# A pre-norm attention and feed-forward block on one core: the first slot's order of maxima, LayerNorm, value products and small transposes

## The chip, the cores and the metric

The kernel runs on one core of one Trainium2 chip. The metric is the device time of one execution in microseconds. The numbers are float32 throughout.

## The reference

For 4 sequences (batches) of 512 tokens and width 512: LayerNorm, attention with 32 query heads of 16 columns in groups of four that share 8 key and value heads, rotary embedding, a causal softmax, an output product, a residual sum, then LayerNorm again, a gated feed-forward layer of 1376 columns and a second residual sum.

```python
q = q * cos + _rotate_half(q) * sin
k = k * cos + _rotate_half(k) * sin
att = jnp.einsum('bhgqd,bhkd->bhgqk', qg, k) / math.sqrt(D_HEAD)
att = jnp.where(causal, att, -jnp.inf)
probs = jax.nn.softmax(att, axis=-1)
ctx = jnp.einsum('bhgqk,bhkd->bhgqd', probs, v)
...
x = x + attention(_layernorm(x), Wq, Wk, Wv, Wo)
x = x + (silu(xt @ W_gate.T) * (xt @ W_up.T)) @ W_down.T   # xt = _layernorm(x)
```

## The kernel before

**Order.** Every engine executes its instructions in the order in which the program issues them; no planner moves them. Tiles of a pool are reused in turn, and an instruction that needs a tile, or a bank of the accumulator memory (PSUM), waits until its last reader is done. The SyncE queue (SP) issues all loads concerned here.

**Banks.** Of the eight PSUM banks four hold scores (two pairs, `pairs[0]` and `pairs[1]`), one the value products (`av`), and three go in turn to everything else through `bank()` (L160): projections, transposes, the feed-forward layer.

**Head groups.** The 32 heads of a batch are cut into 8 groups of 4 heads. The softmax needs the row maximum ahead of the exponential, so each group's scores are computed twice. `scores` (L436) makes them row by row in three rounds; after each round `greatest` copies pair 1 to SBUF on ScalarE (`copy`, L447) and takes the maxima on VectorE, of pair 0 from PSUM, then of pair 1 from the copy (L454). `lowered` (L471) transposes the maxima on TensorE and VectorE adds them to the queries (`qa`, L472). `lowered_scores` (L480) makes the transposed scores with the maximum taken off, ScalarE takes the exponential into `e` (`probabilities`, L487), GpSimd (POOL) masks it (L491), and `averages` (L509) multiplies by the values.

**The pipeline.** The loop in `slot` runs over a batch's 8 groups. While group g has its lowered scores, exponentials and value products, group g+1 has its scores and maxima, in the same four banks. Between these steps `gap()` puts work of other stages, from a list of steps with costs: after gap n the cost done is the sum of the first n shares. In slot 0 the list holds the projections of batches 1, 2 and part of 3; in later slots the feed-forward layer of the batch before.

**The steps of a projection.** `begin` loads the input tiles (L243) and puts LayerNorm items on the deque `aside`; `norm` takes statistics on VectorE (L175 to L177), a power on POOL (L178) and scales on VectorE (L183). `do(aside)` issues one such item. `turned` transposes the normalised tiles (L195) and copies them to `xnT`, on VectorE (L198) for odd tiles and ScalarE (L200) for even ones. A product (L220; L275 for values) comes in two halves from `halved`; after the second, `finish` reads the bank at once: for queries and keys `rotated` (L228 and L230 on VectorE, L229 and L231 on POOL), for keys also `spread` (L260, L262, by way of `aside`), for values a copy on ScalarE (L284). `masked` (L421) makes `qa` on POOL.

**Prologue.** Ahead of slot 0 the program loads batch 0 and the weights, makes batch 0's keys, queries and values, and the first group's scores and maxima. `later` and `later_act` hold the scaling of finished groups (L519 to L533).

Of the kernel before, what the change touches and what calls it, by code (L numbers as in the profile page):

```python
# [21 lines left out]
P = 128  # L22
# [52 lines left out]
def preln_block_kernel(  # L75
# [81 lines left out]
    def load_w(t, src):  # L157
        nc.sync.dma_start(out=t, in_=src.rearrange("(k p) m -> p k m", p=P))

    def bank():  # L160
        return ps_mm.tile([P, T], F32, tag="mm", name="mm")

# [29 lines left out]
    def transposed(xn, i, xnT):  # L192
        pt = bank()
        for k in range(NK):
            nc.tensor.transpose(pt[:, ts(k, P)], xn[:, ts(k, P)], ident)  # L195
        src = pt.rearrange("p (k q) -> p k q", k=NK)
        if i % 2:
            nc.vector.tensor_copy(xnT[:, :, ts(i, P)], src)  # L198
        else:
            nc.scalar.copy(xnT[:, :, ts(i, P)], src)  # L200

    def halved(products, finish):

        made = {}

        def one():
            made["ps"] = bank()
            for step in products[: len(products) // 2]:
                step(made["ps"])

        def two():
            for step in products[len(products) // 2 :]:
                step(made["ps"])
            finish(made["ps"])

        return one, two
# [223 lines left out]
    def greatest(g, at, lo, hi):  # L440
# [6 lines left out]
        nc.scalar.copy(copy[:, :, lo:hi], pairs[1][:, :, lo:hi])  # L447
        for pair, src in enumerate((pairs[0], copy)):
            for i, c in at:
                n = P * (i + 1)  # L450
                for r in range(2):
# [10 lines left out]
                        accum_out=low[hf][:, i, row : row + 1],  # L462
                    )

    def lowered(g):
# [77 lines left out]


    for i in range(NT):
        load_xr(0, i)
    load_w(wk_sb, wk)
    nc.sync.dma_start(out=rope_sb, in_=rope)
    load_w(wq_sb, wq)
    load_w(wv_sb, wv)  # L550
    load_w(wo_sb, wo)

# [4 lines left out]
    begin[1]()  # L557
    do(aside, len(aside))
    for t in low:
        nc.gpsimd.memset(t, 0.0)  # L560
    for n in range(4):
        nc.gpsimd.memset(values(n), 1.0)
    for cost, step in turned:
        step()
    begin1[1]()
    for cost, step in start[:4]:
        step()
# [4 lines left out]
    rounds = (((3, 0),), 0, T), (((2, 0), (0, 3 * P)), 0, T), (((1, 2 * P),), 2 * P, T)  # L572
    scores(0, rounds[0][0])
    greatest(0, *rounds[0])
    do(aside, 3)
    for cost, step in start[6:8]:
        step()
    scores(0, rounds[1][0])
    greatest(0, *rounds[1])
    do(aside, 2)  # L580
    for cost, step in (turned1[0], *start[8:10], turned1[1]):
        step()
    scores(0, rounds[2][0])
    greatest(0, *rounds[2])
    for cost, step in (*turned1[2:], *start[10:]):
        step()
    masked(1)
    lowered(0)

    def fill(steps, upto, done):  # L590
# [6 lines left out]
    def slot(b, steps):  # L597
# [3 lines left out]

        shares = [0.19, 0.17, 0.19, 0.2, 0.25]
        done, part, n = 0.0, 0.0, 0

        def gap():
            nonlocal done, part, n
            part += shares[n % 5]
            n += 1
            done = fill(steps, total * part / 8, done)

        for g in range(8 * b, 8 * b + 8):
# [4 lines left out]
            do(later)  # L616
            do(aside)
            gap()
# [8 lines left out]
            do(later)  # L627
            do(aside)
            gap()
            at, lo, hi = rounds[1]  # L630
            scores(g + 1, at)
            greatest(g + 1, at, lo, hi)
            gap()
            at, lo, hi = rounds[2]
# [5 lines left out]
            gap()  # L640
            lowered(g + 1)
            averages(g)
        for cost, step in steps:
# [16 lines left out]

    slot(0, [begin2, *rest1, *turned2, begin3, *rest2, *turned3, *rest3[:-4]])

# [60 lines left out]
```

## Time and profile before

| | |
|---|---|
| median of 3 runs | 989.39 us (989.32 to 993.88) |
| profiled execution | 993.68 us, of which the span 992.0 |
| TensorE busy | 926.5 us (93%), mean granted clock 0.979 |
| VectorE busy | 535.8 us (54%) |
| ScalarE busy | 296.6 us (30%) |
| GpSimd busy | 216.0 us (22%) |

The engines' busy times are sums over the whole span, in which stages with different limits follow one another. In the page's slices the span is cut into 40 parts of 24.8 us, each digit the busy share in tenths. The prologue ends at 52.6 us of the span and slot 0 at 225.3; slots 1 to 3 and the last feed-forward layer follow. PE is TensorE, DVE VectorE, ACT ScalarE, POOL GpSimd. In an answer in order of time a row has start and duration in us, engine, line, operation, output and inputs; in brackets, the idle time of the engine before it and what ended it.

### The profile page before, as it was taken

The page shows a single profiled execution, that of the slowest core. Times are in us where ns is not written, and L with a number is a line of the kernel's source. Part 1 is how long each engine was busy: PE and PEld are TensorE (multiplying, and loading weights), DVE is VectorE, ACT ScalarE, POOL GpSimd, SP SyncE. Part 2 cuts the span into 40 slices and gives each one's busy share as a digit, 9 for nine tenths or more (in the row PEclk, how much of TensorE's full clock was granted, in tenths as well). Part 3 has the DMA queues.
Part 4 walks back from the last instruction along what each step waited for, and adds up shares of the span by engine and source line. Part 5 has one row for each costly group of instructions (what it writes and reads, how often), then busy time and mean ns, then how long its engine had stood idle before and what let it go on. Part 6 is the DMA issues. An engine that isn't in the chain of part 4 may idle for free.

```text
span 992.0 us, 12710 instructions
## 1 busy us (share of the span) xinstructions
PE 926.5 (93%) x4800; PEld 412.3 (42%) x4800; DVE 535.8 (54%) x1488; ACT 296.6 (30%) x385; POOL 216.0 (22%) x291
## 2 busy tenths in 40 slices
PE   6779887889899999999999999999999999999998
PEld 3334343443344444444444444444444443444443
DVE  5766677767665656475555564655655553312110
ACT  0134344443334333333333433323333431010000
POOL 5353354443311111212111111111111111100000
PEclk9898899999899999999999999999999999999999
DMA  6100100000244310040112110101212102022100
GB/s 212 43 1 1 34 11 1 2 1 1 65 159 126 84 45 26 11 170 11 53 45 53 43 50 11 54 1 43 54 43 54 41 19 64 11 75 75 47 11 32
DMA packets 56813, 46.63 MB, mean 47 GB/s; under 512 B 6352, under 2 KB 48336, under 8 KB 56496
## 3 DMA queue, kind: packets, MB, share of 16 engines
q1 hardware_dynamic: 56464, 40.05, 13.9%
q10 hardware_dynamic: 288, 5.77, 1.5%
q8 instruction: 38, 0.62, 0.3%
q14 instruction: 23, 0.19, 0.1%
HBM read 38.73 MB, written 7.08 MB: 46 GB/s over the span
## 4 chain that ended last, share of the span: by engine, by line
PE 77%; DVE 10%; ACT 5%; issue 2%; POOL 1%; DVEq 0%; ACTq 0%; POOLq 0%
PE mm L375 31%; PE mm L401 15%; PE sc L480 8%; PE av L509 8%; PE sc L436 7%; DVE junk L454 6%; PE mm L327 5%; ACT e L487 5%; PE mm L471 1%; PE mm L220 1%; DVE inv L532 1%; DVE st L175 0%; PE mm L195 0%; ACT xnT L200 0%; DVE inv L528 0%
## 5 line engine op out<-in xcount | busy, mean ns | idle before, releaser
L375 PE MATMUL mm<-xnT,shared 128*128 128x512 f32 (+1 forms) x704 | 324.2, 606 | 2.5 <-ACT xnT L200 2.5
L487 ACT ACTIVATE e<-sc 128x1024 f32<-128x1024 f32 (+1 forms) x192 | 160.6, 881 | 281.0 <-PE sc L480 268.0
L454 DVE CUSTOM_DVE_ANT_0 junk<-sc,mask 128x512 f32<-128x512 f32 (+3 forms) x256 | 125.6, 490 | 130.7 <-PE sc L436 94.1
L491 POOL TENSOR_SCALAR_AFFINE_SELECT e<-e 128x512 f32<-128x512 f32 x128 | 83.9, 667 | 512.8 <-issue 240.6
L375 PEld LDWEIGHTS mm<-xnT,shared 128*128 128x128 f32 (+1 forms) x704 | 126.2, 188 | 166.5 <-issue 159.0
L401 PE MATMUL mm<-wd_sb,home 128*128 128x512 f32 (+1 forms) x352 | 158.5, 599 | 0.0
L454 DVE CUSTOM_DVE_ANT_0 junk<-copy,mask 128x512 f32<-128x512 f32 (+3 forms) x256 | 131.2, 513 | 19.7 <-DVE low L454 0.5
L447 ACT COPY copy<-sc 128x1024 f32<-128x1024 f32 (+1 forms) x96 | 83.6, 871 | 194.7 <-PE sc L436 172.0
L480 PE MATMUL sc<-qa,home 32*128 32x512 f32 (+3 forms) x1024 | 96.3, 468 | 12.4 <-DVE low L454 10.2
L436 PE MATMUL sc<-home,qa 32*128 32x512 f32 (+3 forms) x1024 | 94.3, 460 | 10.7 <-ACT e L487 10.0
L401 PEld LDWEIGHTS mm<-wd_sb,home 128*128 128x128 f32 (+1 forms) x352 | 64.9, 190 | 82.7 <-issue 81.6
L509 PE MATMUL av<-e,home 128*32 128x512 f32 (+3 forms) x1024 | 80.7, 459 | 0.0
L480 PEld LDWEIGHTS sc<-qa,home 32*128 32x128 f32 x1024 | 43.3, 184 | 81.6 <-DVE low L454 54.3
L384 DVE SCALAR_TENSOR_TENSOR g<-g,mm 128x512 f32<-128x512 f32 (+1 forms) x44 | 30.2, 686 | 86.5 <-ACT g L383 86.5
L436 PEld LDWEIGHTS sc<-home,qa 32*128 32x128 f32 x1024 | 47.2, 187 | 64.8 <-issue 21.0
L327 PE MATMUL mm<-wo_sb,cx 128*128 128x512 f32 x128 | 62.0, 623 | 5.7 <-POOL cx L533 5.7
L220 PE MATMUL mm<-xnT,shared 128*128 128x512 f32 x120 | 62.2, 655 | 1.7 <-DVE xnT L198 0.9
L386 DVE TENSOR_TENSOR home<-mm,g 128x512 f32<-128x512 f32 (+1 forms) x44 | 30.4, 690 | 52.8 <-PE mm L375 52.7
L383 ACT ACTIVATE g<-mm 128x512 f32<-128x512 f32 (+1 forms) x44 | 26.3, 598 | 100.9 <-PE mm L375 100.9
L532 DVE RECIPROCAL inv<-inv 128x256 f32<-128x256 f32 x32 | 55.3, 1739 | 0.1
L405 DVE SCALAR_TENSOR_TENSOR xr<-mm,xr 128x512 f32<-128x512 f32 x16 | 11.0, 690 | 78.7 <-PE mm L401 78.7
L509 PEld LDWEIGHTS av<-e,home 128*32 128x32 f32 x1024 | 30.0, 114 | 40.2 <-issue 37.6
(70 smaller groups left out, 561.3 us busy)
## 6 DMA issues: line engine op xcount, KB each, us to landing
shared<-in_wg SPq DMA_DIRECT2D x40, 256.0 KB, 2.8
shared<-in_wu SPq DMA_DIRECT2D x40, 256.0 KB, 2.9
xr<-in_x SPq DMA_DIRECT2D x16, 256.0 KB, 3.5
out<-xr SPq DMA_DIRECT2D x16, 256.0 KB, 2.0
xa<-in_x SPq DMA_DIRECT2D x12, 256.0 KB, 2.8
spill<-wd_sb ACTq DMA_DIRECT2D x1, 2816.0 KB, 9.0
home<-spill ACTq DMA_DIRECT2D x1, 2816.0 KB, 12.5
wd_sb<-in_wd SPq DMA_DIRECT2D x1, 2560.0 KB, 10.8
```

Source lines behind the costliest of these rows:

```text
L220: nc.tensor.matmul(ps, lhsT=w[:, k, ts(m, P)], rhs=xnT[:, k, :], start=k == 0, stop=k == NK - 1)
L327: nc.tensor.matmul(ps, lhsT=cx[m][:, ts(i, P)], rhs=wo_sb[:, m, :], start=m == 0, stop=m == 3)
L375: nc.tensor.matmul(ps[:m, :], lhsT=wgu[c][:, a, k, :m], rhs=xnTs[""][:, k, :], start=k == 0, stop=k == NK - 1)
L401: nc.tensor.matmul(py[i], lhsT=homes[n][:m, f, ts(i, P)], rhs=wd_sb[:m, f, :], start=f == 0, stop=f == NF - 1)
L436: nc.tensor.matmul(sc[r][:, c : c + n], lhsT=qa[g][rows, ts(i, P)], rhs=k[rows, :n], start=True, stop=True)
L447: nc.scalar.copy(copy[:, :, lo:hi], pairs[1][:, :, lo:hi])
L454: nc.vector.tensor_tensor_reduce(out=junk[:, :n], in0=src[:, r, c : c + n], in1=mask[:, T - n :], scale=-1.0, scalar=BIG, op0=ALU.add, op1 ...
L480: nc.tensor.matmul(sc[r][:, c : c + T - P * j], lhsT=k[rows, ts(j, P)], rhs=qa[g][rows, P * j :], start=True, stop=True)
L487: nc.scalar.activation(e[:, 2 * n : 2 * n + 2, :], pairs[n][:, :, :width], AF.Exp, scale=1.0 / math.sqrt(DH))
L491: nc.gpsimd.affine_select(out=e[:, :, c : c + P], in_=e[:, :, c : c + P], compare_op=ALU.is_ge, fill=0.0, base=0, pattern=[[0, 4], [1, P]] ...
L509: nc.tensor.matmul(av[32 * r : 32 * r + 32, P * j :], lhsT=v[:, j, 4 * (m // 2) + r, DH * (1 - hf) : DH * (3 - hf)], rhs=e[:, r, c : c + n ...
L532: nc.vector.reciprocal(r, r)
```

## The change

In a mode `thin`, on from batch 0's first scores to the end of slot 0, the following is done.

- `finish` of a projection is not issued after its second half but put on a deque `full`. It is issued by `greatest`, after pair 0's maxima in the first and second round, after pair 1's in the third; or by `bank()`, which issues the oldest while more than one is waiting.
- LayerNorm items are issued after the first and the second round's maxima and at the group's end, no longer after the first and second exponential.
- `averages` goes ahead of `lowered`, and a sixth gap follows `lowered`, with shares of its own.
- All copies of transposed tiles are on ScalarE.

In the prologue, batch 1's input is loaded ahead of wv; wq is loaded in two parts, the first 128 columns early, the rest after wv; batch 1's LayerNorm is issued after the first half of batch 0's key product, with three of the four memsets on POOL behind it; batch 1's transposes and key product come after the third maxima; and batch 0's last query product follows `lowered(0)`. The work done is the same.

```diff
+    full = deque()
+    thin = [True]
+
     def bank():
+        while len(full) > 1:
+            full.popleft()()
         return ps_mm.tile([P, T], F32, tag="mm", name="mm")
...
-        if i % 2:
+        if i % 2 and not thin[0]:
             nc.vector.tensor_copy(xnT[:, :, ts(i, P)], src)
...
-            finish(made["ps"])
+            if thin[0]:
+                full.append(lambda: finish(made["ps"]))
+            else:
+                finish(made["ps"])
...
-        for pair, src in enumerate((pairs[0], copy)):
+        def maxima(pair, src):
             for i, c in at:
...
+        maxima(0, pairs[0])
+        if lo == 0:
+            do(full, len(full))
+        maxima(1, copy)
+        do(full, len(full))
...
     load_w(wk_sb, wk)
     nc.sync.dma_start(out=rope_sb, in_=rope)
-    load_w(wq_sb, wq)
-    load_w(wv_sb, wv)
-    load_w(wo_sb, wo)
+    load_columns(wq_sb, wq, 0, P)
...
     begin[1]()
     do(aside, len(aside))
+    begin1[1]()
+    load_w(wv_sb, wv)
+    load_columns(wq_sb, wq, P, D)
+    load_w(wo_sb, wo)
     for t in low:
         nc.gpsimd.memset(t, 0.0)
-    for n in range(4):
-        nc.gpsimd.memset(values(n), 1.0)
+    nc.gpsimd.memset(values(0), 1.0)
+    thin[0] = False
     for cost, step in turned:
         step()
-    begin1[1]()
-    for cost, step in start[:4]:
+    for cost, step in start[:1]:
+        step()
+    do(aside, len(aside))
+    for n in range(1, 4):
+        nc.gpsimd.memset(values(n), 1.0)
+    for cost, step in start[1:4]:
         step()
...
+    thin[0] = True
+    for at, steps in zip(rounds, ([*start[6:8]], [*start[8:10]], [*turned1, *rest1[:2]])):
+        scores(0, at[0])
+        greatest(0, *at)
+        for cost, step in steps:
+            step()
     masked(1)
     lowered(0)
+    for cost, step in start[10:]:
+        step()
...
-        shares = [0.19, 0.17, 0.19, 0.2, 0.25]
+        shares = [0.17, 0.15, 0.17, 0.17, 0.17, 0.17] if b == 0 else [0.19, 0.17, 0.19, 0.2, 0.25]
+        thin[0] = b == 0
...
             do(later)
-            do(aside)
+            if not thin[0]:
+                do(aside)
...
             greatest(g + 1, at, lo, hi)
+            if thin[0]:
+                do(aside)
             gap()
...
-            lowered(g + 1)
-            averages(g)
+            if thin[0]:
+                averages(g)
+                lowered(g + 1)
+                do(aside)
+                gap()
+            else:
+                lowered(g + 1)
+                averages(g)
+        thin[0] = False
+        do(full, len(full))
...
-    slot(0, [begin2, *rest1, *turned2, begin3, *rest2, *turned3, *rest3[:-4]])
+    slot(0, [begin2, *rest1[2:], *turned2, begin3, *rest2, *turned3, *rest3[:-4]])
```

In the prologue before, the three rounds of group 0 were written out: after the first `do(aside, 3)` and the second query product; after the second `do(aside, 2)`, two transposes of batch 1 around the third query product; after the third the other two transposes and the fourth query product; then `masked(1)` and `lowered(0)`.

More of the change, by code (lines that the diff above doesn't have):

```diff
@@ L542, in preln_block_kernel, with load_columns @@
     HOME = {0: 0, 1: 1, 2: 2, 3: 1}
+    def load_columns(t, src, lo, hi):
+        nc.sync.dma_start(out=t[:, :, lo:hi], in_=src[:, lo:hi].rearrange("(k p) m -> p k m", p=P))
     for i in range(NT):
@@ L572, in preln_block_kernel @@
     rounds = (((3, 0),), 0, T), (((2, 0), (0, 3 * P)), 0, T), (((1, 2 * P),), 2 * P, T)
[L573 to L586, printed above, removed]
+    thin[0] = True
[4 more added lines that the diff above has]
+            step()
     masked(1)
     lowered(0)
+    for cost, step in start[10:]:
+        step()
     def fill(steps, upto, done):
@@ L600, in slot @@
         total = sum(cost for cost, _ in steps)
-        shares = [0.19, 0.17, 0.19, 0.2, 0.25]
+        shares = [0.17, 0.15, 0.17, 0.17, 0.17, 0.17] if b == 0 else [0.19, 0.17, 0.19, 0.2, 0.25]
         done, part, n = 0.0, 0.0, 0
+        thin[0] = b == 0
         def gap():
             nonlocal done, part, n
-            part += shares[n % 5]
+            part += shares[n % len(shares)]
             n += 1
@@ L627, in slot @@
             do(later)
-            do(aside)
+            if not thin[0]:
+                do(aside)
             gap()
@@ L640, in slot @@
             gap()
-            lowered(g + 1)
-            averages(g)
+            if thin[0]:
+                averages(g)
+                lowered(g + 1)
+                do(aside)
+                gap()
[4 more added lines that the diff above has]
+        do(full, len(full))
         for cost, step in steps:
```

## The prediction

> **What bounds the kernel now.** I read the page's slices first, then a table by stretch, one stretch for each head group of the first slot, then TensorE's waits there, then the order of time. The slices show where there is something to gain: PE, TensorE's busy tenths, is 6 to 9 in the first nine slices (24.8 us each) and 9 almost everywhere after; the granted clock below it dips in the same slices.
> ```profile
> PE   6779887889899999999999999999999999999998
> ...
> PEclk9898899999899999999999999999999999999999
> ```
> The table by stretch (columns: stretch, length, then busy us and instructions of PE, PE's weight loads, DVE, ACT, POOL, the clock, DMA share, GB/s) says that no engine is full in the first slot. The last row is the first group of slot 1.
> ```profile
> 52.50:76.30 23.80, 19.48 (x116) 7.96 (x116) 15.64 (x49) 7.58 (x9) 14.76 (x17) 0.86 0.00 1
> ...
> 142.70:163.80 21.10, 16.26 (x144) 9.18 (x144) 18.30 (x52) 8.17 (x10) 11.60 (x15) 1.00 0.00 1
> 163.80:183.70 19.90, 17.15 (x132) 7.86 (x130) 12.83 (x42) 9.26 (x12) 9.36 (x11) 1.00 0.00 1
> ...
> 227.00:251.50 24.50, 23.24 (x132) 9.89 (x130) 17.69 (x47) 7.15 (x9) 5.32 (x8) 1.00 0.00 1
> ```
> So a chain bounds it. TensorE's waits from 50 to 227 us (total, times, longest) name its links: score maxima, exponentials, and the maxima again ahead of the small transposes (L471).
> ```profile
> PE sc L480 <- DVE low L454: 10.0, 7, 2.0
> PE sc L436 <- ACT e L487: 7.9, 14, 2.1
> PE mm L471 <- DVE low L454: 7.3, 6, 1.8
> ```
> The groups begin (first L480) at 52.56, 76.36, 96.62, 120.97, 142.60, 163.77, 183.59, 205.74, and slot 1 at 225.31: 172.75 us. I cut a group into three: (a) from there to R1, VectorE's first maximum of the second round: 10.8 in group 5; (b) from R1 to the last maximum of the third, VectorE without a gap: 174.65 to 180.55, 5.9; (c) the tail to the next group, 2.8, shown for group 4:
> ```profile
> 159.94 0.60 ACT L487 ACTIVATE e<-sc 128x512 f32<-128x512 f32 x1 [0.64 <-DVE low L454]
> ...
> 160.61 0.83 POOL L491 TENSOR_SCALAR_AFFINE_SELECT e<-e 128x512 f32<-128x512 f32 x1 [5.06 <-ACT e L487]
> ...
> 161.00 0.55 PE L471 MATMUL mm<-ident,low 128*128 128x128 f32 x3 [0.90 <-DVE low L454]
> ...
> 161.48 2.36 PE L509 MATMUL av<-e,home 128*32 128x512 f32 x32
> ...
> 163.77 1.14 PE L480 MATMUL sc<-qa,home 32*128 32x512 f32 x8
> ```
> The reader is to see that the third exponential of pair 0 waits for VectorE, and that its mask on POOL ends at 161.44, 0.5 after the last maximum (160.95). Today L471 runs in that time.
>
> [...]maxima of pair 1 read `copy` and `mask`, both in SBUF, and the 384-column one, 0.56 elsewhere, takes 1.67 when POOL's rotation starts first:
> ```profile
> 196.43 1.26 POOL L231 TENSOR_TENSOR kr<-kr,rot 128x512 f32<-128x512 f32 x1
> 196.44 1.67 DVE L454 CUSTOM_DVE_ANT_0 junk<-copy,mask 128x384 f32<-128x384 f32 x1
> ```
> [...]half an idle window is enough (columns: stretch, length, PE busy, clock):
> ```profile
> 69.05:72.46 3.41, 1.71 (x7) 1.00 0.02 5
> 72.46:75.87 3.41, 3.41 (x33) 0.59 0.01 2
> ```
>
> **The change, part by part.** Prices from the trace: rotation on VectorE (L228, L230) 1.21 to the next instruction; a LayerNorm item 1.0 (statistics), 0.5 (scaling) or 1.5 (both); spread 0.65; a reciprocal 1.7; half a projection on TensorE 1.8.
>
> Loads. SP gets batch 1's four inputs ahead of wv, three quarters of wq, and wo. They need tiles that batch 0's transposes free at 7.4, 8.8, 10.3 and 12.0, so those weights are issued after 12. At 2.5 to 8.5 us to landing wv is there by 21 for 22.5, wq for 28; wo is needed in slot 1. Nothing. Batch 1's LayerNorm, 6.3 us of VectorE, moves to 12.7-19.1, where VectorE idled 6.6 us for the key product (19.3): nothing, if the last tile lands by 16.7 (12.3 plus 2.5 to 4.3; 8.5 would cost 4). Three memsets of 1.4 on POOL now end at about 22.8 instead of 16.0 and hold the first spread (22.2): first scores +0.5, at 27.4.
>
> Prologue after that: q1 to 32.1, second scores to 33.2, maxima, q1's rotation between them, third maxima to 41.2, q2's rotation to 42.4 (POOL's collision taken as 1.0). Four transposes want three banks; banks are handed out in the order given back:
> ```profile
> 43.90 1.11 PE L195 MATMUL mm<-ident,xa 128*128 128x128 f32 x4 [1.49 <-DVE home L230]
> ```
> There a transpose waited for a rotation's bank although ScalarE had emptied another at 43.0. So the third transpose waits for q2's rotation, TensorE idle from 38.7 to 42.5; then copies to 44.4, batch 1's keys to 48.0, L471, q3 to 52.1. With a slow window (0 to 1.7, taken 0.85[...]) slot 0 begins at 52.95: **+0.4**, with 3.4 us of keys done early.
>
> Where fillers fall. The costs and shares in the code, added up by hand, put today a half projection into the last gap, ahead of L471, in every group; afterwards that gap is empty (but for a transpose in groups 2 and 5) and the new one, between L471 and the next group, is full in all eight. Four halves a group stay.
>
> (a) The second LayerNorm item of a group, today ahead of R1, goes (groups 0 and 4: R1 late by 1.8 with a spread, 1.5), as does 0.8 in group 3. Rotations behind the first round's first maxima (groups 0, 2, 3, 5, 7) use the 3.1 us in which VectorE waits for second scores; only group 2, with a reciprocal, exceeds it: 1.2 + 1.0 + 1.7 - 3.1 = 0.8.
>
> (b) Rotations behind the second round's first maxima (groups 0, 1, 2, 6) and LayerNorm items behind that round (0: 1.0, 1: 1.5, 3: 1.5, 4: 0.5; 6: a spread) lie in the stretch where VectorE has no gap. A rotation costs 1.2 and its collision: POOL's multiply still has 0.9 to run when pair 1's maxima start, its addition takes 1.27; so 0 to 2.1, taken **1.0**. Queued behind them: third maxima, transposes, next group.
>
> (c) Value products first: three quarters run early, the last waits for POOL's mask. From the last maximum: 0.5, last quarter 0.46, L471 0.6, filler 1.8: 3.3 against 2.8. The addition to qa (0.7) hides behind the filler.
>
> Groups, a + b + c: 10.7+9.1+3.3 = 23.1; 10.7+9.6+3.3 = 23.6; 11.5+8.1+3.3 = 22.9; 10.7+7.4+3.3 = 21.4; 10.8+6.4+3.3 = 20.5; 10.7+5.9+3.4 = 20.0; 10.7+8.8+3.3 = 22.8; 10.7+5.9+3.3 = 19.9. Sum 174.2. Before the last quarter TensorE stands b - 4.6: 4.5, 5.0, 3.5 and 4.2 in groups 0, 1, 2, 6, so four slow windows, 0 to 1.7 each, taken 0.85: +3.4. Slot 0: 177.6, **+4.9** on 172.75 (which holds today's slow windows). Transposes' copies all on ScalarE (0.6 each, on an engine less than half busy): nothing. Slots 1 to 3 keep their code and are full with products: nothing.
>
> Sum +5.3. The profiled execution took 993.68 (span 992.0), 0.43% above the median of 989.39; so 999.0 for such an execution, **994.7** for the median.
>
> **Rivals.**
> A, faster: in the collision VectorE goes first and POOL waits. For it: here the maximum took its usual 0.56 and two POOL instructions of 0.77 took 2.21; against it the line at 196.44.
> ```profile
> 67.11 0.56 DVE L454 CUSTOM_DVE_ANT_0 junk<-copy,mask 128x384 f32<-128x384 f32 x1
> 67.15 2.21 POOL L262 TENSOR_SCALAR home<-ks,rope_sb 128x512 f32<-128x512 f32 x2
> ```
> Then five rotations on slot 0's path (four in b, the excess in a) cost 4.8 less, the prologue 1.0 less[...]: 5.3 - 8.4 = -3.1, **986.3**. It decides from about 0.5 us a collision: below that the sum is under zero.
> B, no change: 0.5 a collision and half the slow windows: 5.3 - 2.9 - 2.1, **989.7**.
> C, slower still: 2.1 a collision, full slow windows: 5.3 + 6.4 + 4.2, **1005**.
> D, banks not in that order: the prologue's transposes don't wait, slot 0 begins at 48.4, 4.5 earlier: 5.3 - 4.5, **990.2**. With A it is 5.3 - 4.8 - 1.7 - 4.5 = -5.7, **983.7**.
>
> **Chances.** About 0.5% (4.9 us) is what a measurement of this kernel can tell from no change. My forecast and C 0.40; A with D, or A with fewer slow windows than today (their cost in today's tails is some 5 us), 0.29; A alone, B and D 0.31. The forecast lies just beyond that bound; its own range is 990 to 1003. The range of 980 to 1003 takes in A with D and 4 us below it for the clock, and stops short of C's end; 2 in 10 lie outside. Faster 0.29, same 0.31, slower 0.40.
>
> **What would show it.** Right: slot 0's groups of 22 to 24 us in 0, 1, 2 and 6; L509 waiting for POOL's mask; pair 1's maxima over 0.9 us behind a rotation; L195 waiting for L230 near 40 us. Wrong: groups under 20.5 throughout, or L509 without a wait. VectorE waiting for a load near 13 us would put the loss in the prologue.

## The result, and the profile after

The changed kernel takes **1025.13 us** (median of 4 runs, 1023.92 to 1028.48) against 989.36 for the kernel before: ratio 1.0359, 95% interval 1.034 to 1.0378. It is slower by 3.6%; the prediction was 994.7, with a range up to 1003. The profiled execution has a span of 1022.1 us and a mean granted clock of 0.968 (before: 0.979). Of the runs below one execution, the one that was profiled for e1, ran at a mean clock of 0.655 and took 1358.19 us; it is left out, and nothing is read from its profile.

First the slices of the page after, TensorE's busy tenths and granted clock in 40 equal parts, here of 25.6 us:

```profile
PE   6867767777989999999999999999999999999998
...
PEclk9988889888999999999999999999999999999999
```

The loss lies in the first ten slices: there the clock now reads 8 seven times instead of three, and TensorE's busy digits are lower. After that both kernels look alike. The groups of slot 0 begin at 49.58, 75.97, 103.36, 129.97, 158.36, 184.85, 209.37 and 236.77, and slot 1 at 258.07. So **slot 0 starts 3.0 us earlier than before and takes 208.5 us instead of 172.75**; from slot 1 to the end there are 764.0 us, before 766.7. The table by stretch of the kernel after (stretch, length, busy us and count of TensorE, its weight loads, VectorE, ScalarE, POOL, then clock, DMA share, GB/s), groups 0, 4 and 6 of slot 0, then the first of slot 1:

```profile
49.60:75.90 26.30, 18.42 (x141) 10.87 (x140) 17.70 (x48) 7.59 (x9) 16.49 (x17) 0.87 0.00 1
...
158.40:184.80 26.40, 18.73 (x129) 8.80 (x128) 16.47 (x47) 8.07 (x10) 7.12 (x9) 0.87 0.00 1
...
209.40:236.70 27.30, 19.47 (x117) 8.45 (x116) 17.52 (x43) 8.30 (x11) 10.23 (x12) 0.81 0.00 1
...
258.10:284.00 25.90, 23.46 (x116) 9.91 (x119) 18.97 (x50) 7.59 (x9) 7.88 (x10) 1.00 0.00 1
```

Still no engine is full in slot 0, and the clock there is now 0.81 to 0.93. TensorE's waits from 49 to 258 us (total, times, longest) name the link:

```profile
PE av L524 <- POOL e L506: 37.8, 8, 6.4
PE sc L495 <- DVE low L463: 13.6, 10, 1.6
PE sc L445 <- ACT e L502: 2.9, 10, 0.6
```

A wait that did not exist before, value products (L524) for POOL's mask (L506), comes once in each of the eight groups, 4.7 us on average. The waits on exponentials fell from 7.9 to 2.9, and the small transposes, now L486, wait for nothing. Group 4's end on TensorE, in order of time:

```profile
172.29 1.93 PE L524 MATMUL av<-e,home 128*32 128x512 f32 x24
179.42 1.08 PE L524 MATMUL av<-e,home 128*32 128x256 f32 x8 [5.21 <-POOL e L506]
180.44 1.12 PE L486 MATMUL mm<-ident,low 128*128 128x128 f32 x4
181.34 3.58 PE L229 MATMUL mm<-xnT,shared 128*128 128x512 f32 x4
184.85 1.14 PE L495 MATMUL sc<-qa,home 32*128 32x512 f32 x8
```

and on POOL:

```profile
176.18 1.26 POOL L238 TENSOR_TENSOR rot<-rot,rope_sb 128x512 f32<-128x512 f32 x1 [5.89 <-DVE rot L237]
177.52 1.26 POOL L240 TENSOR_TENSOR home<-home,rot 128x512 f32<-128x512 f32 x1
178.73 0.64 POOL L506 TENSOR_SCALAR_AFFINE_SELECT e<-e 128x512 f32<-128x512 f32 x1
```

The third exponential of pair 0 was ready at 175.04 (ScalarE's L502, 174.44 plus 0.60). Its mask begins only at 178.73, because two instructions of a rotation stand ahead of it in POOL's queue; that rotation was put on `full` and issued behind the third maxima, ahead of the mask. Meanwhile TensorE stands still for 5.2 us. What follows then runs at half clock: L486 takes 1.12 and the half projection 3.58, for about 0.6 and 2.0 at full clock. The clock by windows of 3.41 us around that wait (TensorE busy and count, ..., clock):

```profile
171.00:174.41 3.41, 3.01 (x40) 1.40 (x40) 3.12 (x15) 1.09 (x2) 0.00 (x0) 1.00 0.00 0
174.41:177.82 3.41, 0.00 (x0) 0.00 (x0) 2.08 (x7) 0.60 (x1) 1.57 (x2) 1.00 0.00 0
177.82:181.23 3.41, 1.81 (x12) 1.00 (x13) 0.00 (x0) 0.00 (x0) 2.22 (x3) 0.51 0.00 0
181.23:184.64 3.41, 3.41 (x6) 1.13 (x4) 2.35 (x2) 0.00 (x0) 0.00 (x0) 0.50 0.00 0
184.64:188.05 3.41, 3.27 (x13) 0.99 (x12) 0.00 (x0) 1.93 (x2) 0.00 (x0) 0.98 0.00 0
```

One idle window is followed by two at half clock, the second of them fully busy.

The other difference is the collision of VectorE and POOL, of which the kernel before has less. Group 6 on VectorE, pair 1's second maxima, with `copy` and `mask` in SBUF, each 0.56 when alone:

```profile
224.34 1.28 DVE L463 CUSTOM_DVE_ANT_0 junk<-copy,mask 128x384 f32<-128x384 f32 x1
225.67 1.50 DVE L463 CUSTOM_DVE_ANT_0 junk<-copy,mask 128x384 f32<-128x384 f32 x1
```

They lie beside the rotation on POOL (223.93 to 226.75). All maxima of slot 0 take 80.8 us of VectorE, 67.9 before.

### The profile page after: what moved, and what is told of

Same layout as the page of the kernel before. It is cut to its first block, busy times and chain, and to the rows that moved or that the text cites. A ratio compares the mean times of both kernels' runs of the same rounds, so it can differ in the third digit from the quotient of the medians.

```text
span 1022.1 us, 12707 instructions
## 1 busy us (share of the span) xinstructions
PE 932.1 (91%) x4800; PEld 417.5 (41%) x4800; DVE 546.9 (54%) x1482; ACT 299.6 (29%) x391; POOL 219.2 (21%) x291
## 3 DMA queue, kind: packets, MB, share of 16 engines
q1 hardware_dynamic: 56992, 40.05, 13.5%
## 4 chain that ended last, share of the span: by engine, by line
PE 78%; DVE 10%; ACT 5%; issue 3%; POOL 3%; DMA 0%; SPq 0%; ACTq 0%; DVEq 0%; POOLq 0%
PE mm L384 30%; PE mm L410 14%; PE sc L495 8%; PE sc L445 7%; PE av L524 6%; DVE junk L463 6%; PE mm L336 5%; PE mm L229 4%; ACT e L502 4%; PE mm L486 2%; PE mm L284 1%; DVE inv L547 1%; POOL e L506 1%; PE mm L201 1%; DVE st L181 1%
## 5 line engine op out<-in xcount | busy, mean ns | idle before, releaser
L502 ACT ACTIVATE e<-sc 128x1024 f32<-128x1024 f32 (+1 forms) x192 | 160.5, 881 | 310.0 <-PE sc L495 284.2
L506 POOL TENSOR_SCALAR_AFFINE_SELECT e<-e 128x512 f32<-128x512 f32 x128 | 83.3, 663 | 513.1 <-issue 239.0
L463 DVE CUSTOM_DVE_ANT_0 junk<-copy,mask 128x512 f32<-128x512 f32 (+3 forms) x256 | 145.3, 568 | 18.3 <-ACT home L293 0.5
L524 PE MATMUL av<-e,home 128*32 128x512 f32 (+3 forms) x1024 | 80.3, 450 | 37.8 <-POOL e L506 37.8
L495 PE MATMUL sc<-qa,home 32*128 32x512 f32 (+3 forms) x1024 | 100.1, 485 | 14.7 <-DVE low L463 13.8
L229 PE MATMUL mm<-xnT,shared 128*128 128x512 f32 x120 | 65.6, 684 | 0.8 <-issue 0.8
L524 PEld LDWEIGHTS av<-e,home 128*32 128x32 f32 x1024 | 28.5, 111 | 78.4 <-POOL e L506 40.3
L395 DVE TENSOR_TENSOR home<-mm,g 128x512 f32<-128x512 f32 (+1 forms) x44 | 30.4, 690 | 52.7 <-PE mm L384 52.7
## 6 DMA issues: line engine op xcount, KB each, us to landing
wd_sb<-in_wd SPq DMA_DIRECT2D x1, 2560.0 KB, 10.6
```

What stands on the lines that cost most here:

```text
L229: nc.tensor.matmul(ps, lhsT=w[:, k, ts(m, P)], rhs=xnT[:, k, :], start=k == 0, stop=k == NK - 1)
L463: nc.vector.tensor_tensor_reduce(out=junk[:, :n], in0=src[:, r, c : c + n], in1=mask[:, T - n :], scale=-1.0, scalar=BIG, op0=ALU.add, op1 ...
L495: nc.tensor.matmul(sc[r][:, c : c + T - P * j], lhsT=k[rows, ts(j, P)], rhs=qa[g][rows, P * j :], start=True, stop=True)
L502: nc.scalar.activation(e[:, 2 * n : 2 * n + 2, :], pairs[n][:, :, :width], AF.Exp, scale=1.0 / math.sqrt(DH))
L506: nc.gpsimd.affine_select(out=e[:, :, c : c + P], in_=e[:, :, c : c + P], compare_op=ALU.is_ge, fill=0.0, base=0, pattern=[[0, 4], [1, P]] ...
L524: nc.tensor.matmul(av[32 * r : 32 * r + 32, P * j :], lhsT=v[:, j, 4 * (m // 2) + r, DH * (1 - hf) : DH * (3 - hf)], rhs=e[:, r, c : c + n ...
```

## The experiments

All ratios are to the kernel before, run on the same chip, with 95% intervals. Theory at the outset: the wait on the mask, made by late rotations in POOL's queue, by collisions and by an empty gap ahead of the value products, with the slow clock behind each wait.

The profiles also differ outside slot 0. Everything behind it, which no edit touches, takes 763.3 to 768.8 us, and with the changed prologue slot 0 begins anywhere from 48.75 to 52.91. Where a difference of a few us matters, the length of slot 0 is given beside the median.

### Taking one part back out of the changed kernel

**Tail and gaps as before** (e1):
```diff
-        shares = [0.17, 0.15, 0.17, 0.17, 0.17, 0.17] if b == 0 else [0.19, 0.17, 0.19, 0.2, 0.25]
+        shares = [0.19, 0.17, 0.19, 0.2, 0.25]
...
+            lowered(g + 1)
+            averages(g)
             if thin[0]:
-                averages(g)
-                lowered(g + 1)
                 do(aside)
-                gap()
-            else:
-                lowered(g + 1)
-                averages(g)
```


> The kernel after, with the group's tail and the gaps of slot 0 as before: small transposes ahead of the value products, five gaps with the old shares; finishes and LayerNorm stay where the change put them. Theory (TensorE stands before the last quarter of the value products, for the mask on POOL, and its clock then halves): the mask ends beside the small transposes again, tails fall from 52 us in the eight groups to about 25 to 30, slot 0 from 208.5 to about 181, total about 998. Rival (the loss is VectorE's longer stretch of maxima, rotations and LayerNorm, whatever stands at the tail): slot 0 stays over 198, total over 1015.

Measured 1010.82 us (three executions), 1.0206 (1.0179 to 1.0234): between the two theories. The order of value products and transposes, together with its gap and the gaps' shares, is worth some 14 us in the changed kernel. It is not the whole loss, nor nothing.

**The third round's finishing behind the mask** (e2; in the prologue the same call stands behind `greatest`):
```diff
         maxima(1, copy)
-        do(full, len(full))
+        if lo == 0:
+            do(full, len(full))
...
             masked(g + 2)
+            do(full, len(full))
             gap()
```


> The kernel after, but the finishes that wait for the third round's maxima are issued behind the third exponential, its mask and the next group's qa instead of ahead of them. Nothing else differs. Theory (in groups 3, 4 and 5 a rotation's two instructions stand ahead of the mask in POOL's queue): their tails of 8.7, 9.4 and 8.0 fall by 2.5 to 3.5 each, the other groups stay, total about 1015 to 1017. Rival (the wait is the third exponential's, the mask's place in the queue does not count): within 2 of 1025.

Measured 1012.26, 1.0226 (1.021 to 1.0241). Groups 3 to 5 take 24.9, 21.6 and 19.8 instead of 28.4, 26.5 and 24.5; waits on the mask fall to 27.4. POOL's queue is a cause, worth 13 us, more than expected, as the slow clock behind the waits goes with it. But removing it leaves 23.

**Finishing at once** (e3; the deque `full` serves the prologue alone, `inslot` is set when slot 0 begins):
```diff
-            if thin[0]:
+            if thin[0] and not inslot[0]:
                 full.append(lambda: finish(made["ps"]))
```


> The kernel after, but in slot 0 a product's finish is issued at once after its second half, as before; LayerNorm's place, the value products' place and the six gaps stay. Theory: rotations leave the stretch between the second and third maxima in groups 0, 1, 2 and 6 (about 3 each with the collisions of VectorE and POOL), and in groups 3 to 5 they stand earlier in POOL's queue than the mask by a round (about 3 each, less 2 for VectorE); total 1007 to 1013. Rival (the order of value products alone costs, as the mask comes last whatever else is done): 1018 or more.

Measured 1011.08, 1.0211 (1.0191 to 1.0231): the total is as the theory had it. By group it is less tidy: groups 1, 2, 3, 5 and 6 take 2.7 to 4.0 us less than in the changed kernel, but 0 and 4 only 0.5, and 25.0 us of waits on the mask stay.

**LayerNorm where it was** (e7; the same edit after both exponentials, and the two new calls taken out):
```diff
             do(later)
-            if not thin[0]:
-                do(aside)
+            do(aside)
             gap()
...
                 lowered(g + 1)
-                do(aside)
                 gap()
```


> The kernel after, but with slot 0's LayerNorm items issued where they were before (behind the first exponential, the first maxima and the second exponential). Theory (LayerNorm behind the second maxima adds 4.5 us to the stretch of maxima in five groups, and gives some of it back ahead of the second round): 1020 to 1024. Rival (it is LayerNorm that makes the third exponential late): under 1015.

Measured 1023.59, 1.0344 (1.0328 to 1.0359). LayerNorm's place is minor: the 1.5 us less than the changed kernel lie within the two intervals.

### Keeping TensorE busy, and leaving POOL's half out

**Value products three times** (e5; the first three quarters of them are issued three times):
```diff
+        early3 = [(0, e0, 0), (1, e1, 0), (3, e1, 3 * P)]
-        for j, e, c in ((0, e0, 0), (1, e1, 0), (3, e1, 3 * P), (2, e2, 0)):
+        for n_, (j, e, c) in enumerate((*(early3 * (3 if thin[0] else 1)), (2, e2, 0))):
```


> The kernel after, but in slot 0 the first three quarters of a group's value products (24 instructions, 1.9 us) are issued three times, so that 3.9 us of extra products stand where TensorE waits for the mask (3.4 to 6.4 us in groups 0 to 6, 1.5 in group 7). They are summed three times, which changes the values. Theory (a wait of 4 us and more halves the clock for the tail behind it): tails fall by about 2.3 in seven groups, group 7 grows by 2.4, total about 1011 although TensorE does 31 us more. Rival (the slow tails have another cause, or the extra work delays what follows): 1024 or more.

Measured 1018.06, 1.0292 (1.0266 to 1.0317): 7 us faster than the changed kernel *with 384 more matmuls*, between theory and rival. Its slot 0 takes 196.3, 12.2 less, at a clock of 0.97 instead of 0.85. In this profile slot 0 begins 3.3 us later than in the changed kernel's, and what lies behind slot 0 takes 3.2 longer, which is why the run gains less than the slot. In the changed kernel seven of the waits on the mask, of 3.37 to 6.41 us, have half clock behind them (L486 at 1.12), and the eighth, of 1.55, has not (0.66). The slow clock behind the waits is thus a cost of its own, some 12 us of slot 0's 36.

**POOL's half of the rotation left out** (e6, slot 0 only):
```diff
-        engine.tensor_tensor(rot, rot, sin, ALU.mult)
+        if not inslot[0]:
+            engine.tensor_tensor(rot, rot, sin, ALU.mult)
         nc.vector.tensor_tensor(dst, ps, cos, ALU.mult)
-        engine.tensor_tensor(dst, dst, rot, ALU.add)
+        if not inslot[0]:
+            engine.tensor_tensor(dst, dst, rot, ALU.add)
```


> The kernel after, but in slot 0 the rotation leaves out its two instructions on POOL (product with the sines and sum), so queries and keys made there are not rotated. VectorE's two stay, all orders stay. Theory (POOL's half of the rotation costs twice: ahead of the mask in its queue in groups 3 to 5, and by holding VectorE's maxima of pair 1 in groups 0, 1, 2 and 6, about 2 each, which also shortens waits and so slow windows): about 1000. Rival (only the queue counts): as with the mask ahead of the finish, 1010 to 1014.

Measured 999.1, 1.0092 (1.0074 to 1.0109), as expected. POOL's half of the rotation is worth 26 us in the changed kernel, through collision and queue together; 19.9 us of waits on the mask stay. This is not the price of its late place: the kernel before, whose rotations have that half too, was not run without it, and finishing at once (e3) gained 14.

### One part alone on the kernel before

**The changed prologue alone** (e4; slot 0 in the old order, batch 1's keys out of its list):
```diff
-        shares = [0.17, 0.15, 0.17, 0.17, 0.17, 0.17] if b == 0 else [0.19, 0.17, 0.19, 0.2, 0.25]
+        shares = [0.19, 0.17, 0.19, 0.2, 0.25]
...
-        thin[0] = b == 0
+        thin[0] = False
+        do(full, len(full))
```


> The changed prologue alone (loads, batch 1's LayerNorm, transposes and key product early, finishes waiting for maxima there); slot 0 in the order of before, with its shares and without batch 1's key product. Theory: the 3.0 us by which slot 0 began earlier stay, 985 to 987. Rival (slot 0 is bound by its chain and gives back what the prologue won, or meets a bank or tile in use): 989 or more.

Measured 996.59, 1.0068 (1.0051 to 1.0085): the theory was wrong. Work done earlier made the kernel slower. TensorE's waits in slot 0:

```profile
PE sc L495 <- DVE low L463: 15.5, 13, 1.6
PE mm L486 <- DVE low L463: 11.1, 6, 3.2
```

Against the kernel before (10.0 and 7.3) both grew. In this profile slot 0 takes 176.8 us, 4.1 more than before although batch 1's keys are gone from it, and begins at 52.49, no earlier than before; why the start of slot 0 moves is shown under "Prologue" further below.

**Value products first, the sixth gap and its shares alone** (e8):
```diff
-        shares = [0.19, 0.17, 0.19, 0.2, 0.25]
+        shares = [0.17, 0.15, 0.17, 0.17, 0.17, 0.17] if b == 0 else [0.19, 0.17, 0.19, 0.2, 0.25]
...
-            lowered(g + 1)
-            averages(g)
+            if b == 0:
+                averages(g)
+                lowered(g + 1)
+                gap()
+            else:
+                lowered(g + 1)
+                averages(g)
```


> The kernel before, with one part of the change alone: in slot 0 value products ahead of the small transposes, the sixth gap behind them, and its shares. Finishes at once, LayerNorm and prologue as before. Theory (the last quarter waits for the mask whatever the rest does, and the clock halves behind the wait): tails of 5 to 6 us instead of 2.9, less what the slow windows of today cost, total 1004 to 1012. Rival (it costs only together with the finishes behind the maxima): under 996.

Measured 987.62 (20 runs), 0.9985 (0.9976 to 0.9994): the theory was wrong again. The order that seemed to make the loss costs nothing by itself. Its waits on the mask:

```profile
PE av L509 <- POOL e L491: 3.4, 2, 1.9
```

Two, not eight. The timeline shows why: in six of the eight groups a half projection stands *ahead of* the value products, in the gap after the third maxima, and runs while the mask is made. In the changed kernel that gap is empty, but for a transpose in groups 2 and 5. The two kernels have the same shares, but not the same list: with batch 1's key product done in the prologue, the later steps fall into other gaps. That was the new theory, tried next.

### Where the list falls into the gaps

**The changed kernel with batch 1's keys back in slot 0's list** (e9):
```diff
-    for at, steps in zip(rounds, ([*start[6:8]], [*start[8:10]], [*turned1, *rest1[:2]])):
+    for at, steps in zip(rounds, ([*start[6:8]], [*start[8:10]], [*turned1])):
...
-    slot(0, [begin2, *rest1[2:], *turned2, begin3, *rest2, *turned3, *rest3[:-4]])
+    slot(0, [begin2, *rest1, *turned2, begin3, *rest2, *turned3, *rest3[:-4]])
```


> The changed kernel with batch 1's key product put back into the first slot's list, so that the prologue holds only batch 1's transposes ahead of it. The list then falls into the gaps as in the earlier run that changed the order alone: the gap between the third maxima and the value products holds a half projection in most groups, and most last gaps are empty. Everything else is as changed. Theory (the mask on POOL is exposed because that gap is empty, and the deferred rotations land in the gap ahead of the third maxima): about 995 to 1003 us, slot 0 at 178 to 186 us, TensorE's waits on the mask under 12 us in all. Rival (it doesn't matter where the list's steps fall): 1020 us or more, slot 0 at 205 us or more less 3 for nothing saved.

Measured 1006.42, 1.0177 (1.0145 to 1.0209): 18.7 us faster than the changed kernel, though its slot 0 has 3.4 us more work. The waits on the mask fall to 15.5. The expected 995 to 1003 was too good, but half of the loss hangs on the place of this one product. That it acts by the gap ahead of the value products is argued from the waits on the mask (37.8 before the edit, 15.5 behind it); no run moves one filling alone and leaves the rest of the list in place.

**The changed prologue, the old order, keys in the list** (e10: e4 with the same two lines):


> The kernel before with the changed prologue, slot 0's order as before, and batch 1's key product left in slot 0's list (the earlier run of the changed prologue alone had it in the prologue and took 996.6 us). Theory (that run lost its time because the list, shorter by the keys, fell otherwise into the gaps, with rotations between the second and third maxima): 985 to 989 us, slot 0 from its begin to slot 1 within 2 us of the 172.75 us of the kernel before. Rival (the new prologue itself costs): 994 us or more.

Measured **985.98**, 0.9954 (0.9937 to 0.9971), as the theory had it. Between e4 and e10 lie 10.6 us, by the place of one key product; the waits of small transposes on the maxima fall from 11.1 to 5.6. In the profiles slot 0 takes 171.2 us, 5.7 less than in e4 although it has the key product again. The changed prologue without that product gains: slot 0 begins at 49.20, 3.4 us earlier than before. The two waits of batch 1's transposes on LayerNorm, 0.98 and 2.89 us in the kernel before, are gone.

### What finishing late costs, and by which way

**Value products first and finishing behind the maxima** (e11: e8, with `full` used in slot 0):
```diff
-            finish(made["ps"])
+            if thin[0]:
+                full.append(lambda: finish(made["ps"]))
+            else:
+                finish(made["ps"])
...
+        maxima(0, pairs[0])
+        if lo == 0:
+            do(full, len(full))
+        maxima(1, copy)
+        do(full, len(full))
```


> The kernel before with value products ahead of the small transposes and the sixth gap (the earlier run of that alone took 987.6 us), and with it the finishing of a projection behind the maxima, in slot 0; LayerNorm and the prologue as before. Theory (the finishing behind maxima costs most where the mask is exposed, and here the gap ahead of the value products is full): 990 to 1000 us. Rivals: no cost at all, 989 us or less; or the whole cost of the changed kernel less its prologue, 1010 us or more.

Measured 1010.27, 1.0201 (1.0183 to 1.0219), the costly rival: late finishing alone takes 22.6 us from e8, even though the gap ahead of the value products is filled.

**The same with finishing behind pair 1's maxima in every round** (e13):
```diff
         maxima(0, pairs[0])
-        if lo == 0:
-            do(full, len(full))
         maxima(1, copy)
         do(full, len(full))
```


> The kernel before with value products first, the sixth gap, and finishing behind the maxima (1010.3 us in that form), but with the finishing issued behind pair 1's maxima in every round instead of between pair 0's and pair 1's in the first two. The instructions are the same; POOL's half of a rotation then runs beside maxima that read PSUM. Theory (collision): pair 1's maxima of 512 and 384 columns fall from 1.34 and 1.08 us to about 0.75, VectorE's time in the maxima of slot 0 from 83.8 to 67 to 70 us, and the run takes 990 to 997 us. Rival (the queue on POOL, or late rotations as such): 1006 us or more.

Measured 1000.98, 1.0116 (1.0102 to 1.0131): between the two. VectorE's maxima in slot 0 fell from 83.8 to 71.2 us (67.9 in the kernel before), so most of the collision is gone, and with it 9.3 us; 13.4 stay. Where some of these come from is to be seen in group 1, VectorE of e13:

```profile
81.85 0.72 DVE L236 STREAM_SHUFFLE rot<-mm 128x512 f32<-128x512 f32 x1
82.47 0.67 DVE L238 TENSOR_TENSOR home<-mm,rope_sb 128x512 f32<-128x512 f32 x1
...
84.07 1.49 DVE L188 TENSOR_SCALAR xa<-xa,mv,rstd 128x512 f32<-128x512 f32 x1
...
87.35 0.54 DVE L462 CUSTOM_DVE_ANT_0 junk<-sc,mask 128x384 f32<-128x384 f32 x1
```

and of e8:

```profile
83.00 0.95 DVE L183 TENSOR_SCALAR xa<-xa,mv,rstd 128x512 f32<-128x512 f32 x1
83.87 0.54 DVE L454 CUSTOM_DVE_ANT_0 junk<-sc,mask 128x384 f32<-128x384 f32 x1
...
90.04 0.74 DVE L228 STREAM_SHUFFLE rot<-mm 128x512 f32<-128x512 f32 x1
90.68 0.67 DVE L230 TENSOR_TENSOR home<-mm,rope_sb 128x512 f32<-128x512 f32 x1
```

In e8 a rotation runs at the group's end, behind the third maxima, while VectorE would wait for the transposes. Put off to the next round, it stands with two LayerNorm items ahead of the second maxima, which begin 14.6 us after the group's start instead of 11.3. About 1.3 us of that is a slow start on TensorE (the first L492 2.09 for 1.14, and the half projection behind it), the rest the rotation and a LayerNorm scaling that meets POOL's half of it (1.49 for 0.54). The group takes 24.8 us instead of 21.0.

**The same edit in the changed kernel** (e14):


> The changed kernel with the finishing behind pair 1's maxima in every round, nothing else. Theory (collision): the maxima lose their 13 us, and the run takes 1005 to 1014 us, with TensorE's waits on POOL's mask as long as in the changed kernel. Rival (the mask's wait behind POOL's queue is the whole loss): 1020 us or more.

Measured 1024.52, 1.0358 (1.0338 to 1.0378): the rival's number. The maxima did lose 12.4 us (80.8 to 68.4), and groups 0 to 2 take 6.5 less in all. Slot 0 takes 5.3 us less, but in this profile it begins 3.3 later and what lies behind it takes 2.0 longer, so the run gains nothing. In group 6 the gain is lost on VectorE itself: the shuffle for the spread (L269), ahead of the third maxima, now waits 2.2 us for POOL's half of the keys' rotation. In group 3 POOL shows what became of it:

```profile
147.56 1.26 POOL L238 TENSOR_TENSOR rot<-rot,rope_sb 128x512 f32<-128x512 f32 x1 [2.17 <-DVE rot L237]
148.90 1.26 POOL L240 TENSOR_TENSOR home<-home,rot 128x512 f32<-128x512 f32 x1
150.12 0.64 POOL L504 TENSOR_SCALAR_AFFINE_SELECT e<-e 128x512 f32<-128x512 f32 x1
```

The maxima are done sooner, and the mask still stands behind the rotation: TensorE waits 7.15 us there, 6.41 in the changed kernel.

**Both: behind pair 1's maxima in rounds one and two, behind the mask in the third** (e15):
```diff
         maxima(0, pairs[0])
+        maxima(1, copy)
         if lo == 0:
             do(full, len(full))
-        maxima(1, copy)
-        do(full, len(full))
...
             masked(g + 2)
+            do(full, len(full))
             gap()
```


> The changed kernel with the finishing of the first two rounds behind pair 1's maxima, and that of the third behind POOL's mask (that alone gave 1012.3 us). Theory (collision and queue are two costs that add up): 996 to 1002 us, about what leaving POOL's half out gave. Rival (they overlap, the one hides the other): 1006 us or more.

Measured 1009.95, 1.021 (1.0197 to 1.0223): the rival's number, but not its reason. The gains of e14 (0.6) and e2 (12.9) add up to 13.5, and both together gain 15.2; in slot 0 alone 5.3 and 13.8 add up to 19.1, and both together gain 21.4. So the two costs do add up, and the collision is the small one here. Slot 0 shrinks to 187.1 (e2: 194.7), but from slot 1 to the end this profile has 768.7 us, against 764.3 in e2. A wait of 6.37 stays in group 6, from a rotation of keys issued in the second round: VectorE waits 2.2 us for POOL's half of it ahead of the third maxima, and the four scalings of its spread on POOL (L271, 3.2 us) make the mask another 1.1 late.

### Versions that might beat both

**e8 with LayerNorm's second item at the group's end** (e12):
```diff
             do(later_act)
             do(later)
-            do(aside)
+            if b > 0:
+                do(aside)
...
                 averages(g)
                 lowered(g + 1)
+                do(aside)
                 gap()
```


> The kernel before with value products ahead of the small transposes and the sixth gap (987.6 us by itself), and the LayerNorm item that stood behind the second exponential moved to the group's end. Theory (that item stood ahead of VectorE's second maxima on the path in about half of the groups, 0.5 to 1.5 us each; at the end it lies beside the last gap's product): 983 to 986 us. Rival (VectorE waited there anyway, or the item now delays the next group's first maxima by as much): 987 to 988 us.

Measured 987.05, 0.9977 (0.9952 to 1.0002): no gain over e8 that the runs can tell, though the profiled execution took 980.84 and its slot 0 162.2 us, the shortest of all. Its 14 runs fall in two bands, 981 to 985 (clock 0.982 to 0.991) and 989 to 993 (0.975 to 0.979).

**The prologue of e10 with the order of e12** (e16: e10, with the shares and the loop's end of e8 and the two edits of e12):


> The parts that gained or cost nothing, together: the changed prologue with batch 1's keys left in slot 0's list (986.0 us by itself), value products ahead of the small transposes with the sixth gap, and LayerNorm's second item at the group's end (987.1 us); finishing at once, as before. If the gains add up: 980 to 984 us. If the prologue's gain needs the old order (the start of slot 0 moves, or the filling falls otherwise): 986 us or more.

Measured 988.92, 0.9976 (0.9958 to 0.9994). The gains don't add up, and again there are two bands, 981.5 to 985 and 987.5 to 990.4 (mean clocks of 0.984 to 0.987 and of 0.977 to 0.980). What makes an execution fall into one or the other stays open. By its median **e10 is the best version found**, 0.5% faster than the kernel before; its interval overlaps those of e12 and e16.

### The loss as a two-by-two

Four of the kernels share the changed prologue's loads, value products first and the sixth gap. They differ in two things (e16 also in where LayerNorm's first item and the odd copies stand; e7 put LayerNorm's place at 1.5 us):

| us | keys in slot 0's list | keys in the prologue |
|---|---|---|
| finishing at once | 988.9 (e16) | 1011.1 (e3) |
| finishing behind the maxima | 1006.4 (e9) | 1025.1 (changed kernel) |

Each of the two costs 14 to 22 us, and together they are the whole 36. The lengths of slot 0 in the profiles show the same pattern: 169.4 (e16), 190.0 (e3), 190.2 (e9) and 208.5 (changed kernel). What is left of the change without these two (e16) comes out within 0.3% of the kernel before.

## Why the prediction was wrong, point by point

The sign came out as the likeliest of the three, at a chance of 0.40, and the wait on the mask is where it was predicted; the size is far off. Two steps failed where it counts. Term (c) let the mask end 0.5 us after the last maximum and let half of the slow windows pass: 29.9 us were predicted for the tails, 52.0 measured. And "3.4 us of keys done early" was put at nothing, though it moves every filling behind it: 18.7 us by e9, which overlap with the tails.

In the span, the prediction had 992.0 + 5.3 = 997.3, and 1022.1 was measured: 24.8 us, of which -3.4 ahead of slot 0, +30.9 in slot 0 (208.5 for 177.6) and -2.7 behind it. (The median misses by 30.4, because the profiled execution of before was 4.3 above its median, and that of after 1.2 below.)

**Prologue, +0.4: wrong, in both directions.** The third transpose was to wait for q2's rotation near 42.5. It ran at 40.26, three us ahead of that rotation (43.24):

```profile
40.26 1.14 PE L201 MATMUL mm<-ident,xa 128*128 128x128 f32 x8 [0.24 <-ACT wd_sb L206]
```

It waits for ScalarE's copy and no rotation. The step that failed is "banks are handed out in the order given back", read from one line of the profile before; by which rule they are handed out stays open. Rival D was right here, slot 0 beginning 3.0 us earlier than before, and e10 shows the gain when nothing eats it.

The other way, batch 1's early LayerNorm was booked as nothing and the first scores at 27.4. The scores came at 28.87, 2.0 us later than before, because the last of the scalings, 0.54 elsewhere, ran beside the moved memsets and held up the key rotation behind it:

```profile
18.39 2.69 POOL L589 MEMSET home<- 128x1536 f32 x2
18.47 2.89 DVE L189 TENSOR_SCALAR xa<-xa,mv,rstd 128x512 f32<-128x512 f32 x1 [0.44 <-POOL rstd L184]
21.29 0.72 DVE L237 STREAM_SHUFFLE rot<-mm 128x512 f32<-128x512 f32 x1
```

TensorE then waits 3.09 us ahead of the first scores (0.62 before). In the profile of the changed kernel the clock stayed full there, and q1's product took 3.70 us. With the same prologue slot 0 begins at 49.65 to 52.88 in e2 to e7, so the changed kernel's 49.58 was luck in part.

**Where the fillers fall: right on the place, wrong on the price.** The gap ahead of the value products was to be empty and the new one full, and so it is. Overlooked was that the gap after the first maxima is now empty too, in all eight groups (before in groups 3 and 7). The reading of the kernel before was off in group 2, whose last gap holds three transposes and no half projection. Of the empty gap I priced four slow windows; and the keys' move to the prologue was booked as "3.4 us of keys done early" with no cost. e9 and e10 show that this very move sets the filling, and costs 18.7 us in the new order, 10.6 in the old.

**(c) Tails: 26.5 + 3.4 predicted, 52.0 measured (before: 28.9). This is the largest miss.** Two of its parts failed.
- *The slow window, 0.85 in four groups.* Groups 0, 1, 2 and 6, without a rotation ahead of the mask in the third round, have tails of 5.7, 5.6, 6.0 and 5.3 for 3.3: 2.35 each. The wait itself was nearly right: 5.6, 5.5, 3.4 and 5.8 for the predicted 4.5, 5.0, 3.5 and 4.2. What it costs is the last quarter at 1.0 for 0.46, L486 at 0.9 for 0.6 and the half projection at 2.8 to 3.6 for 1.8. I took a window of half clock to be hit half of the time, and its end at the next window; in fact all of the tail runs at half clock, and in seven groups. That is 7 x 2.35 - 3.4 = 13 us. The windows above show it for group 4: 0.51 behind the idle window, 0.50 all through the next, in which TensorE was busy for 3.41 of 3.41, and 0.98 only after that. e5 measured 12.2.
- *POOL's queue ahead of the mask.* That the mask ends 0.5 after the last maximum failed in groups 3, 4 and 5, whose tails are 8.7, 9.4 and 8.0. I followed the rotation of the third round on VectorE, behind all maxima, and booked nothing; its half on POOL is issued ahead of the mask, and in group 4 the mask ends 3.9 after the last maximum, 3.4 late. Beyond the 2.35 these tails hold 9 us more than predicted. e2 measured 13, with the slow clock that it saves.

**(a) 86.5 predicted, 92.9 measured (before: 92.1).** Missed was a second slow window. With the gap after the first maxima empty too, TensorE waits 1.6 for pair 0's maxima in every group, and in five of them what follows is slow, here in group 6:

```profile
215.48 2.09 PE L495 MATMUL sc<-qa,home 32*128 32x384 f32 x16 [1.62 <-DVE low L463]
217.50 2.65 PE L229 MATMUL mm<-xnT,shared 128*128 128x512 f32 x4
```

Elsewhere these two take 1.15 and 1.98; groups 1, 2, 3, 6 and 7 are 0.5 to 1.7 longer than predicted. In the window of 3.41 us from 212.06 to 215.47 TensorE was busy for 1.50; in the next, to 218.88, it was busy for 3.40 and its clock was 0.50. Waits of 0.3 and 1.6 us were enough here; both lay in that one window. The two lines from 69.05 on in the prediction had shown as much: busy for 1.71, then a clock of 0.59. In groups 0, 4 and 5, where the same waits fall otherwise into the windows (the emptiest of them was busy for 2.15, 1.77 and 1.76), the two instructions behind them took 1.15 and 1.98.

**(b) 61.2 predicted, 63.6 measured.** The collision, taken as 1.0 between 0 and 2.1, is 1.7: 0.72 and 0.94 on the two maxima of 384 columns above. POOL's multiply began first, at 223.93; VectorE's maximum began at 224.34 and took 1.28. At 196.44 of the profile before a maximum took 1.67, with POOL's addition begun at 196.43. Rival A (VectorE first) did not come. Here the bounds of the prediction held. In e11, where a filled gap hides the mask, the collision was worth 9.3 us (e13); in slot 0 of the changed kernel 5.3 (e14), where the stretch b stays as long as it was (63.2).

**The rivals.** C, at 1005, was closest, and it too took 1.7 for the dearest slow window. A needed VectorE to win the collision; 2.6 of its 8.4 us were slow windows lost by shorter waits, the author's estimate, which no trace shows: group 2's wait of 3.37, the shortest of the seven with a slow tail, still had L486 at 1.12 for 0.66 behind it. B needed half of both costs. Instead slot 0's waits grew: the three largest kinds from 25.2 us (10.0, 7.9, 7.3) to 54.3 (37.8, 13.6, 2.9).

## What to carry to other kernels

A step taken out of a list that fills gaps moves every later step: look at what stands in each gap afterwards, above all in the one that hid a wait, before booking the step as saved. Work that is put off on one engine is put off on every engine that it issues to: write down what stands behind it in each queue, and whether it slows what runs beside it then (here maxima of 0.56 took 1.28 and 1.50). In the profiles before and after, half clock followed every window of 3.41 us in which TensorE was busy for less than 1.42, and lasted to the end of one in which it was busy for 3.04 or more: behind such a wait count what runs up to there at twice its time. How short waits fall into the windows differed from group to group.

## What the runs showed of the hardware that I had not expected

- After an idle window of 3.41 us the clock of the changed kernel was 0.51 and 0.50 for two windows (177.82 to 184.64), the second fully busy: a wait of 5.2 us cost some 2.4 more behind it.
- In the profiles before and after the stretches of half clock begin whole windows of 3.413 us apart. Of 544 such windows at full clock in the two, counted from 20 us on, all 13 with TensorE busy for less than 1.42 us were followed by half clock, 9 of the 12 with 1.42 to 1.77, and none with more. Of 31 windows at half clock, none of the 9 with 2.22 us busy or less ended it, and all 22 with 3.04 or more did.
- A scaling on VectorE of 0.54 us took 2.89 beside memsets on POOL (18.39 to 21.08 of the changed kernel).
- Issuing three quarters of the value products three times made the changed kernel 7 us faster (1018.06 for 1025.13), with slot 0's clock at 0.97 for 0.85.
- Two kernels, e12 and e16, have executions in two bands some 6 to 8 us apart, at the same instructions, with mean clocks of 0.982 to 0.991 in the faster band and 0.975 to 0.980 in the slower.
